# Fetching 32 columns of A per row for list tiles that belong to single groups

## The chip, the cores and the metric

The kernel runs on one core of a Trainium2 chip. The core has five engines with instruction queues of their own: TensorE (PE, with its weight loads shown apart as PEld), VectorE (DVE), ScalarE (ACT), GpSimd (POOL) and SyncE (SP). Sixteen DMA engines move data between the off-chip memory (HBM) and the on-chip memory (SBUF). The accumulators of TensorE lie in PSUM. The metric is the device time of one execution in microseconds (us). Three runs of the kernel before took 1524.8, 1528.96 and 1532.77 us; the median is 1528.96 us.

## The reference

Eight batches of 4096 nodes with 256 features pass through one layer of a graph network, a residual addition and a layer norm. The matrix `A` is 4096 x 4096 and mostly zero: node pairs with small numbers are connected often, those with large numbers rarely.

```python
HW = jnp.einsum('bnf,fo->bno', H, W)
A_norm = jax.nn.relu((A + A.T) * 0.5)
D = jnp.sum(A_norm, axis=1)
d_inv_sqrt = jnp.where(D > 0, D_safe ** (-0.5), 0.0)
DAD = d_inv_sqrt[:, None] * A_norm * d_inv_sqrt[None, :]
L_norm = jnp.eye(N, dtype=H.dtype) - DAD
out = jax.nn.relu(jnp.einsum('nm,bmo->bno', L_norm, HW))
x = _layernorm(x + out)
```

## The kernel before

**First stage, up to about 594 us.** The matrix is read in blocks of 512 x 512. TensorE transposes a block, VectorE adds it to its mirror block, ScalarE halves it and takes the positive part (`symmetrise` L464, `keep` L475). The result goes to `a_dram`, a table in HBM with 4096 rows of 4096 float32 values. VectorE also sums each row over groups of 32 columns (`sums`, L479, three buffers), and GpSimd notes in `uses` (L480) which groups of which rows hold anything. For blocks on the diagonal GpSimd copies the diagonal tile away (`diag`, L489). Beside this, TensorE forms the products of x and W, which are scaled by each row's root of the degree and written to `g_dram`: 4096 rows of 8 batches x 256 values, 8 KB each. `a_dram` and `g_dram` have one row more, of zeros, for places in a list that stay empty. The first 128 output rows are computed here with dense products (`lead`, L536).

Constant tables are filled at the very start. GpSimd writes the tables `kinds`, `limit` and `base` with one memset for every column (L184, L187, L188): 14 of the first and 224 of each other.

**Second stage.** The other 31 blocks of 128 output rows are handled in 16 units `u`, in the order `SEQ` (1 to 7, 0, 8 to 15). A unit has two blocks, `b` = 0 and 1 (output blocks 2u+1 and 2u+2); the last has one. A unit's 256 columns of A are eight groups of 32 (`E` = 32). Only rows of A that hold something in these columns have to be multiplied. They are sorted by the pattern of groups in which they hold something, the kinds: a kind is a mask of eight bits. The kinds 1, 2, 4, 8 (in block 0) and 16, 32, 64, 128 (in block 1) are single groups; 15 and 240 are a whole block; 51, 204, 60 and 195 are the same or crossed halves of both blocks; kind 0 takes the rest and needs all groups. Each kind has room for `CAPS[u][k]` slots of 64 rows, beginning with slot `FIRST[u][k]`. Two slots make a list tile of 128 rows. There are 268 list tiles, 10 to 27 to a unit. The rows 0 to 255 of A, which almost every column uses, are not listed: they are kept as `hubs` and multiplied whole (`gh`, L902).

The list of a unit is built on the chip, four units ahead of its use, mostly on VectorE (`patterns` L214, `place` L267, `place_rest` L350, `spread` L374). Its last steps are `collect` (L398), in which TensorE writes for every place of every tile the number of the row, in two parts, to PSUM, and `index` (L409), in which VectorE turns these into `gi`, the row of `g_dram`, and `ai`, the place in `a_dram`. `ai` is written in up to three pieces (L429) by the bounds of L123: first the tiles whose columns lie in block 0, then those of block 1, then those that need both. In the function `lists` (L1064) the steps of three units are put behind one another: `index` of one, then the scans of `place_rest` and of `place` of two later ones, which read the rest of the two PSUM banks that `lists` has borrowed from the accumulators of block 0. VectorE works through them in this order.

`gather` (L907) fetches a tile with two indirect DMAs on GpSimd's queue: the tile's columns of A into `ga` (L914) and its rows of g into `g` (L922). A row of `ga` is 128 columns (512 bytes), or 256 columns (1 KB) when both blocks need it. There is a ring of 12 buffers of each kind; `gather_ahead` (L932) issues the next pair as soon as the oldest tile's last product is behind. For most units the tiles of the next one are therefore on their way while this one is multiplied.

TensorE follows a list of 227 steps written out beforehand (`steps_of`, L789). A full step multiplies 128 rows by the 128 columns of one block, in four pieces of 512 values of g. A round has up to eight operations, each 64 rows by one group of 32 columns, by the same four pieces; the two halves of the rows and the four column groups lie side by side in the array. `product` (L1115) issues each matmul; its weights are `at[ps, off + cols.start : off + cols.stop]`, so a group's 32 columns are taken from the fetched 128 or 256.

When a block is done, ScalarE evicts it with the positive part and the row's factor (L731), VectorE adds x (L741), forms the statistics and normalises (L750 to L774), and SyncE's queue stores it. x is loaded from ScalarE's queue (L725) into four buffers, which the stores set free.

Of the kernel before, what the change touches and what calls it, by code (L numbers as in the profile page):

```python
# [2 lines left out]

# [8 lines left out]
ALU = mybir.AluOpType  # L12
AX = mybir.AxisListType
BF16 = mybir.dt.bfloat16
# [7 lines left out]
KINDS = [15, 1, 4, 2, 8, 16, 64, 32, 128, 240, 51, 204, 60, 195, 0]  # L22

SEQ = [1, 2, 3, 4, 5, 6, 7, 0, *range(8, 16)]
# [3 lines left out]
CAPS = [  # L28
# [18 lines left out]
FIRST = [  # L47
# [20 lines left out]
def kernel(  # L68
# [25 lines left out]
    nc = tc.nc  # L94
    B, N, F = x.shape
    FO = w.shape[1]
    P = 128
# [3 lines left out]
    NB = N // P  # L101
    FC = F // P
    G = B * FO
    NU = NB // 2
    Q = 64
    E = 32
    QU = P // E
    NE = 2 * QU
# [5 lines left out]
    NK = len(KINDS)  # L114
    L = 64
    mid = KINDS.index(16), KINDS.index(51)
    NL = NK - 1

    def upto_tile(u, ks):
        return max((FIRST[u][k] + CAPS[u][k] + 1) // 2 for k in ks)  # L120

    tiles = [upto_tile(u, range(NK)) for u in range(NU)]
    bounds = [(upto_tile(u, range(mid[0])), upto_tile(u, range(mid[1]))) for u in range(NU)]  # L123
    tmax = max(tiles)

    const = ctx.enter_context(tc.tile_pool(name="const", bufs=1))
# [15 lines left out]
    a_dram = dram.tile([N + 1, N], F32, name="a_dram")  # L142
# [42 lines left out]
    for u in SEQ:  # L185
        for k in range(NL):
            nc.gpsimd.memset(limit[:, u, k : k + 1], float(CAPS[u][k] * L))  # L187
            nc.gpsimd.memset(base[:, u, k : k + 1], float(FIRST[u][k] * L + 1))  # L188

    own = const.tile([P, NE, 2], F32, name="own")  # L190
    nc.vector.memset(own, 0.0)
    for s in range(NE):
        h = slice((s % QU) * E, (s % QU + 1) * E)
        nc.vector.memset(own[h, s, s // QU : s // QU + 1], 1.0)
    over = const.tile([P, NU], F32, name="over")

    def blocks(u):

        return min(2, NB - 1 - 2 * u)

    plan = {}

# [206 lines left out]
    def index(u, pl):  # L409
        t = tiles[u]  # L410

        low = ipool.tile([P, tmax], F32, tag="low", name=f"low_{u}")
        nc.vector.tensor_copy(low[:, :t], pl[:, 1, :])  # L413
        nc.vector.scalar_tensor_tensor(low[:, :t], pl[:, 0, :], float(P), low[:, :t], ALU.mult, ALU.add)
        gi = ipool.tile([P, tmax], U32, tag="gi", name=f"gi_{u}", bufs=3)
        nc.vector.tensor_scalar(gi[:, :t], low[:, :t], float(N), None, ALU.add)

        ai = ipool.tile([P, tmax], U32, tag="ai", name=f"ai_{u}", bufs=3)
        m0, m1 = bounds[u]
        if blocks(u) == 1:  # L420
            m0 = m1 = t
        for ts, n, k in (
            (slice(0, m0), NB, 2 * u + 1),
            (slice(m0, m1), NB, 2 * u + 2),
            (slice(m1, t), NU, u),
        ):
            if ts.start == ts.stop:
                continue
            nc.vector.tensor_scalar(  # L429
                ai[:, ts], low[:, ts], float(n), float(N * n + k), ALU.mult, ALU.add  # L430
            )
        plan[u] = gi, ai
        yield

# [8 lines left out]
    with (  # L443
# [219 lines left out]
        for i in range(NS):  # L663
# [37 lines left out]
            if i in (1, 2):  # L701
                for n, u in enumerate(SEQ[2 * i - 2 : 2 * i]):
                    at = 1 + 5 * n
# [79 lines left out]
    def store(i, z):  # L783
        nc.sync.dma_start(out[:, i * P : (i + 1) * P, :].rearrange("b p f -> p b f"), z)

    a_rows = a_dram.rearrange("j (c q) -> (j c) q", q=P)
    a_pairs = a_dram.rearrange("j (c q) -> (j c) q", q=2 * P)

# [67 lines left out]
    with (  # L856
# [8 lines left out]
        hubs = [  # L865
            gath.enter_context(tc.tile_pool(name=f"hub_{h}", bufs=1)).tile([P, G], F32, name=f"g_hub{h}")
            for h in range(max(HUBS))
        ]
        ring_rows = [apool.tile([P, 2 * P], F32, tag=f"a{k}", name=f"ga{k}") for k in range(RING)]
        hub_rows = [  # L870
            [apool.tile([P, P], F32, tag=f"h{h}{b}", name=f"gh{h}_{b}") for b in range(2)] for h in range(max(HUBS))
        ]
# [22 lines left out]
        def load_hub_rows(units, h, b):  # L895

            u = next((v for v in units if HUBS[v] > h), None)
            if u is None:
                return
            i = 2 * u + 1 + b  # L900
            with queue("pool"):
                nc.gpsimd.dma_start(  # L902
                    hub_rows[h][b], a_dram[h * P : (h + 1) * P, i * P : (i + 1) * P]
                )
            got[u, -1 - h, b] = (hub_rows[h][b], hubs[h], 0)

        def gather(n):  # L907

            u, t = order[n]
            both = t >= bounds[u][1]  # L910
            at, gt = ring_rows[n % RING], ring[n % RING]
            gi, ai = plan[u]
            with queue("pool"):
                nc.gpsimd.indirect_dma_start(  # L914
                    out=at if both else at[:, :P],
                    out_offset=None,
                    in_=a_pairs if both else a_rows,
                    in_offset=bass.IndirectOffsetOnAxis(ap=ai[:, t : t + 1], axis=0),
                    element_offset=P if both else 0,
                )  # L920
            with queue("pool"):
                nc.gpsimd.indirect_dma_start(  # L922
                    out=gt,
                    out_offset=None,
                    in_=g_dram,
                    in_offset=bass.IndirectOffsetOnAxis(ap=gi[:, t : t + 1], axis=0),
                    bounds_check=N if n < RING else N - 1,
                    oob_is_err=False,
                )
            got[u, t] = (at, gt, P if both else 0)  # L930

        def gather_ahead():  # L932
            nonlocal asked, eaten
# [181 lines left out]
        def product(u, op, c, ps, cols, start, stop):  # L1115

            t, _, b, _ = op
            at, gt, apart = got[u, t] if t >= 0 else got[u, t, b]
            off = b * apart
            with queue("pe"):  # L1120
                return nc.tensor.matmul(  # L1121
                    py[2 * u + 1 + b][c][cols, :],
                    lhsT=at[ps, off + cols.start : off + cols.stop],
                    rhs=gt[ps, c * S : (c + 1) * S],
                    start=start,
                    stop=stop,
                    skip_group_check=True,
                )
# [138 lines left out]
```

## Time and profile before

| What | Value |
|---|---|
| median of three runs | 1528.96 us |
| the profiled execution | 1529.14 us |
| its span, first to last instruction | 1527.3 us |
| TensorE busy | 1390.9 us (91%) |
| VectorE busy | 1040.8 us (68%) |
| GpSimd busy | 739.9 us (48%) |
| ScalarE busy | 363.7 us (24%) |
| moved by DMA | 550.64 MB, 361 GB/s on average |
| mean granted clock of TensorE | 0.964 of full |

The busy time of an engine is the time in which it has an instruction at work. Matmuls overlap, so a busy TensorE isn't a TensorE at its peak. "PEclk" is the clock granted to TensorE in tenths of full speed, and "DMA" is the mean busy share of the 16 DMA engines, in 40 equal slices of the span. A group row names line, engine, operation, output and inputs, shape and count, then its total time and the mean of one, and then the idle time of the engine before these instructions with what ended it.

### The profile page before, as it was taken

Reading aid. Unit: us, or ns where it says so; the run is one execution under the profiler, and the core shown is the slowest. Engines: PE = TensorE matmul, PEld = TensorE weight load, DVE = VectorE, ACT = ScalarE, POOL = GpSimd, SP = SyncE. Lnnn points to the kernel's source line nnn. Section 1 sums busy time; section 2 is a strip of 40 time slices with the busy share of each in tenths; the row PEclk is TensorE's granted clock in tenths of the full one; section 3 lists DMA queues with packets and bytes.
Section 4 is the critical chain, followed back from the end, with each engine's and each line's share of the span. In section 5 each row is a group of like instructions: output and inputs, shape, how many; then the busy total and the mean of one; then the engine's idle time right before and its main releaser. Section 6 shows DMA issues by size and latency. Waiting matters only on the chain.

```text
span 1527.3 us, 29344 instructions
## 1 busy us (share of the span) xinstructions
PE 1390.9 (91%) x11008; PEld 753.8 (49%) x11008; DVE 1040.8 (68%) x3135; ACT 363.7 (24%) x462; POOL 739.9 (48%) x1264
## 2 busy tenths in 40 slices
PE   6999998989989987999999999999899998989883
PEld 5878877777777752343433333333233333333331
DVE  6676578979955454109586797789109988999354
ACT  3555544544544440000101101100001010101111
POOL 4002010011303324766775776776556776777661
PEclk9999999999999988899999999999899999999996
DMA  9999999999989997998999999999978999999994
GB/s 352 361 362 398 392 371 355 359 350 358 351 308 352 340 403 263 398 411 320 389 366 382 368 391 374 409 368 362 415 269 285 371 392 400 386 380 384 408 364 156
DMA packets 217924, 550.64 MB, mean 361 GB/s; under 512 B 19369, under 2 KB 107737, under 8 KB 183193
## 3 DMA queue, kind: packets, MB, share of 16 engines
q0 software_dynamic: 55392, 290.44, 48.7%
q1 hardware_dynamic: 93472, 126.89, 24.2%
q10 hardware_dynamic: 68912, 131.37, 22.8%
q8 instruction: 89, 1.46, 0.4%
q14 instruction: 59, 0.48, 0.1%
HBM read 445.64 MB, written 136.34 MB: 381 GB/s over the span
## 4 chain that ended last, share of the span: by engine, by line
PE 50%; DMA 23%; DVE 16%; issue 6%; POOL 3%; ACT 2%; SPq 0%; ACTq 0%; POOLq 0%; DVEq 0%
PE py L1121 31%; DMA g<-g_dram,gi 9%; PE pg L578 9%; PE lead L536 5%; DMA a_dram<-sym 4%; DVE sym L472 3%; DMA out_dram<-xr 3%; PE tr L468 3%; DMA xin<-in_x_dram 3%; PE xtr L567 3%; DVE sums L479 2%; DMA ga<-a_dram,ai 2%; POOL ga L914 2%; DMA adj<-in_adj_dram 1%; DVE stats L750 1%
## 5 line engine op out<-in xcount | busy, mean ns | idle before, releaser
L1121 PE MATMUL py<-g,ga 64*32 64x512 f32 (+1 forms) x7136 | 627.0, 608 | 41.3 <-DMA g<-g_dram,gi 34.3
L1121 PEld LDWEIGHTS py<-g,ga 64*32 64x32 f32 (+1 forms) x7136 | 229.2, 113 | 422.8 <-issue 333.8
L922 POOL DMA_INDIRECT g<-g_dram,gi x268 | 299.6, 1118 | 117.5 <-issue 57.6
L914 POOL DMA_INDIRECT ga<-a_dram,ai x268 | 285.6, 1066 | 139.7 <-PE py L1121 69.8
L731 ACT ACTIVATE y<-py,minus_r 128x512 f32<-128x512 f32 x120 | 74.9, 688 | 808.5 <-PE py L1121 608.4
L578 PE MATMUL pg<-w_sb,xt 128*128 128x256 f32 x1024 | 229.2, 382 | 5.8 <-ACT xt L568 4.0
L1121 PE MATMUL py<-g_hub,gh 128*128 128x512 f32 x480 | 220.7, 601 | 5.0 <-DVE pos_k L210 5.0
L472 DVE TENSOR_TENSOR sym<-tr,adj 128x512 f32<-128x512 f32 x256 | 162.1, 681 | 73.9 <-PE tr L468 72.3
L578 PEld LDWEIGHTS pg<-w_sb,xt 128*128 128x128 f32 x1024 | 193.6, 192 | 33.5 <-ACT xt L568 4.4
L480 POOL TENSOR_SCALAR uses<-sums 128x64 uint8<-128x64 f32 x64 | 27.6, 431 | 346.7 <-DVE sums L479 308.4
L479 DVE TENSOR_REDUCE sums<-sym 128x64 f32<-128x2048 f32 x64 | 145.3, 2277 | 54.9 <-ACT sym L476 54.9
L468 PE MATMUL tr<-ident,adj 128*128 128x128 f32 x1024 | 140.3, 288 | 29.5 <-DVE sym L472 16.3
L1121 PEld LDWEIGHTS py<-g_hub,gh 128*128 128x128 f32 x480 | 87.6, 190 | 132.7 <-issue 118.2
L476 ACT ACTIVATE sym<-sym 128x2048 f32<-128x2048 f32 x64 | 122.8, 1918 | 127.5 <-DVE sym L472 127.5
L413 DVE COPY low<-lists 128x17 f32<-128x17 f32 (+8 forms) x14 | 2.4, 174 | 221.1 <-PE lists L401 221.1
L468 PEld LDWEIGHTS tr<-ident,adj 128*128 128x128 f32 x1024 | 120.5, 147 | 56.1 <-DVE sym L472 31.5
L741 DVE TENSOR_TENSOR xr<-xr,y 128x2048 f32<-128x2048 f32 x31 | 70.9, 2286 | 61.4 <-ACT y L731 29.3
L750 DVE BATCH_NORM_STATS2 stats<-xr 128x6 f32<-128x256 f32 x256 | 87.0, 412 | 1.1
L567 PE MATMUL xtr<-ident,xin 128*128 128x128 f32 x512 | 72.1, 290 | 16.5 <-DVE sym L472 14.0
L774 DVE TENSOR_SCALAR xr<-xr,mv,root 128x256 f32<-128x256 f32 x248 | 83.9, 409 | 0.5
L536 PE MATMUL lead<-gt,strip 128*128 128x512 f32 x176 | 82.6, 593 | 0.0
L380 DVE TENSOR_TENSOR hot<-iota_q,at 128x1024 bf16<-128x1024 f32 x64 | 74.4, 1217 | 7.2 <-DMA a_dram<-sym 7.2
(152 smaller groups left out, 1025.9 us busy)
## 6 DMA issues: line engine op xcount, KB each, us to landing
adj<-in_adj_dram SPq DMA_DIRECT2D x64, 1024.0 KB, 11.8
a_dram<-sym ACTq DMA_DIRECT2D x64, 1024.0 KB, 9.7
out_dram<-xr SPq DMA_DIRECT2D x31, 1024.0 KB, 23.4
xr<-in_x_dram ACTq DMA_DIRECT2D x29, 1024.0 KB, 20.4
xin<-in_x_dram SPq DMA_DIRECT2D x44, 512.0 KB, 12.6
g_dram<-gt ACTq DMA_DIRECT2D x22, 1024.0 KB, 8.5
xin<-in_x_dram POOLq DMA_DIRECT2D x20, 512.0 KB
g_dram<-held ACTq DMA_DIRECT2D x10, 1024.0 KB, 11.5
```

The lines of the kernel that those rows point to most:

```text
L468: ins = nc.tensor.transpose(pt[:, c * P : (c + 1) * P], tji[:, c, a * P : (a + 1) * P], ident)
L472: nc.vector.tensor_add(sym[:, a, :], pt, tij[:, a, :])
L476: nc.scalar.activation(sym, sym, AF.Relu, scale=0.5)
L479: nc.vector.tensor_reduce(sums, sym.rearrange("p a (c q) -> p a c q", q=E), AX.X, ALU.add)
L536: nc.tensor.matmul(lead[c], lhsT=strip, rhs=g[:, c * S : (c + 1) * S], start=not done, stop=len(done) == NB - 1, skip_group_check=True,)
L567: nc.tensor.transpose(pt[:, k, c, :], xin[b // H][:, b % H + k, c * P : (c + 1) * P], ident)
L578: ins = nc.tensor.matmul(pg[:, k * FO : (k + 1) * FO], lhsT=xt[:, b + k, c, :], rhs=w_sb[:, c, :], start=(c == 0), stop=(c == FC - 1),)
L750: nc.vector.bn_stats(stats[:, b, :], z[:, b, :])
L774: nc.vector.tensor_scalar(z[:, b, :], z[:, b, :], mv[:, b, 0:1], rstd[:, b : b + 1], ALU.subtract, ALU.mult,)
L914: nc.gpsimd.indirect_dma_start(out=at if both else at[:, :P], out_offset=None, in_=a_pairs if both else a_rows, in_offset=bass.IndirectOff ...
L922: nc.gpsimd.indirect_dma_start(out=gt, out_offset=None, in_=g_dram, in_offset=bass.IndirectOffsetOnAxis(ap=gi[:, t : t + 1], axis=0), boun ...
L1121: return nc.tensor.matmul(py[2 * u + 1 + b][c][cols, :], lhsT=at[ps, off + cols.start : off + cols.stop], rhs=gt[ps, c * S : (c + 1) * S], ...
```

## The change

For each list tile a table made when the program is built, `owner`, says whose columns it holds: 0 or 1 for one block, 2 for both, and 3 (`ALONE`) when every slot of the tile belongs to a kind of a single group. The two slots of such a tile may belong to different groups. 155 of the 268 tiles are of this sort, 45 others hold columns of one block and 68 those of both.

For an `ALONE` tile each place fetches just the 32 columns of its slot's group, 128 bytes, through a view of `a_dram` in pieces of 32 columns. The piece's number within the row differs by half of the tile, so `index` adds it from a new table `group_of` (128 x 16 x 11, bf16), which GpSimd fills at the start: one memset of the whole and 299 memsets of half a column. `ai` is now written in runs of neighbouring tiles of the same sort, 83 pieces over all units in place of 46. The row's offset N (the lists hold j - N) is added in the first operation of `index` and no longer in the third and in each piece of `ai`. In `product` the weights of an `ALONE` tile are the columns 0 to 31 of `ga`. The shapes of the matmuls, the number of gathers and the number of rows stay.

```diff
+    def owners(u, t):
+        kinds_at = [k for k in range(NK) for s in (2 * t, 2 * t + 1) if FIRST[u][k] <= s < FIRST[u][k] + CAPS[u][k]]
+        masks = [KINDS[k] or 255 for k in kinds_at]
+        if all(m & (m - 1) == 0 for m in masks):
+            return ALONE
+        both = blocks(u) == 2
+        return max(2 if both and m & 15 and m >> QU else int(m & 15 == 0) for m in masks)
+    ALONE = 3
+    owner = [[owners(u, t) for t in range(tiles[u])] for u in range(NU)]
+    alone = [[t for t in range(tiles[u]) if owner[u][t] == ALONE] for u in range(NU)]
...
+    group_of = const.tile([P, NU, max(map(len, alone))], BF16, name="group_of")
+    nc.gpsimd.memset(group_of, 0.0)
+    for u in SEQ:
+        for n, t in enumerate(alone[u]):
+            for i in range(2):
+                for k in range(1, 1 + NE):
+                    if FIRST[u][k] <= 2 * t + i < FIRST[u][k] + CAPS[u][k]:
+                        g = QU * (2 * u + 1) + KINDS[k].bit_length() - 1
+                        nc.gpsimd.memset(group_of[i * L : (i + 1) * L, u, n : n + 1], float(g))
...
-        nc.vector.tensor_copy(low[:, :t], pl[:, 1, :])
+        nc.vector.tensor_scalar(low[:, :t], pl[:, 1, :], float(N), None, ALU.add)
         nc.vector.scalar_tensor_tensor(low[:, :t], pl[:, 0, :], float(P), low[:, :t], ALU.mult, ALU.add)
-        nc.vector.tensor_scalar(gi[:, :t], low[:, :t], float(N), None, ALU.add)
+        nc.vector.tensor_copy(gi[:, :t], low[:, :t])
...
+        for who, run_of in groupby(range(t), lambda k: owner[u][k]):
+            run_of = list(run_of)
+            ts = slice(run_of[0], run_of[-1] + 1)
+            if who == ALONE:
+                k = group_of[:, u, n : n + len(run_of)]
+                nc.vector.scalar_tensor_tensor(ai[:, ts], low[:, ts], float(N // E), k, ALU.mult, ALU.add)
+                n += len(run_of)
+            else:
+                rows, k = (NU, u) if who == 2 else (NB, 2 * u + 1 + who)
+                nc.vector.tensor_scalar(ai[:, ts], low[:, ts], float(rows), float(k), ALU.mult, ALU.add)
...
+    a_groups = a_dram.rearrange("j (c q) -> (j c) q", q=E)
     a_rows = a_dram.rearrange("j (c q) -> (j c) q", q=P)
...
+            both, one = owner[u][t] == 2, owner[u][t] == ALONE
...
-                    out=at if both else at[:, :P],
+                    out=at if both else at[:, : E if one else P],
-                    in_=a_pairs if both else a_rows,
+                    in_=a_pairs if both else a_groups if one else a_rows,
...
-            off = b * apart
+            off = -cols.start if one else b * apart
```

More of the change, by code (lines that the diff above doesn't have):

```diff
@@ L1 @@
 from contextlib import ExitStack, nullcontext
-from itertools import chain
+from itertools import chain, groupby
 import concourse.bass as bass
@@ L117, with blocks @@
     NL = NK - 1
+    def blocks(u):
+        return min(2, NB - 1 - 2 * u)
     def upto_tile(u, ks):
@@ L122 @@
     tiles = [upto_tile(u, range(NK)) for u in range(NU)]
-    bounds = [(upto_tile(u, range(mid[0])), upto_tile(u, range(mid[1]))) for u in range(NU)]
+    def owners(u, t):
[8 more added lines that the diff above has]
+    alone = [[t for t in range(tiles[u]) if owner[u][t] == ALONE] for u in range(NU)]
     tmax = max(tiles)
@@ L195 @@
     over = const.tile([P, NU], F32, name="over")
-    def blocks(u):
-        return min(2, NB - 1 - 2 * u)
     plan = {}
@@ L412, in index @@
         low = ipool.tile([P, tmax], F32, tag="low", name=f"low_{u}")
-        nc.vector.tensor_copy(low[:, :t], pl[:, 1, :])
+        nc.vector.tensor_scalar(low[:, :t], pl[:, 1, :], float(N), None, ALU.add)
         nc.vector.scalar_tensor_tensor(low[:, :t], pl[:, 0, :], float(P), low[:, :t], ALU.mult, ALU.add)
         gi = ipool.tile([P, tmax], U32, tag="gi", name=f"gi_{u}", bufs=3)
-        nc.vector.tensor_scalar(gi[:, :t], low[:, :t], float(N), None, ALU.add)
+        nc.vector.tensor_copy(gi[:, :t], low[:, :t])
         ai = ipool.tile([P, tmax], U32, tag="ai", name=f"ai_{u}", bufs=3)
[L419 to L431, printed above, removed]
+        n = 0
+        for who, run_of in groupby(range(t), lambda k: owner[u][k]):
[8 more added lines that the diff above has]
+                nc.vector.tensor_scalar(ai[:, ts], low[:, ts], float(rows), float(k), ALU.mult, ALU.add)
         plan[u] = gi, ai
@@ L904, in load_hub_rows @@
                 )
-            got[u, -1 - h, b] = (hub_rows[h][b], hubs[h], 0)
+            got[u, -1 - h, b] = (hub_rows[h][b], hubs[h], 0, False)
         def gather(n):
             u, t = order[n]
-            both = t >= bounds[u][1]
+            both, one = owner[u][t] == 2, owner[u][t] == ALONE
             at, gt = ring_rows[n % RING], ring[n % RING]
@@ L929, in gather @@
                 )
-            got[u, t] = (at, gt, P if both else 0)
+            got[u, t] = (at, gt, P if both else 0, one)
         def gather_ahead():
@@ L1117, in product @@
             t, _, b, _ = op
-            at, gt, apart = got[u, t] if t >= 0 else got[u, t, b]
-            off = b * apart
+            at, gt, apart, one = got[u, t] if t >= 0 else got[u, t, b]
+            off = -cols.start if one else b * apart
             with queue("pe"):
```

## The prediction

> **What bounds the kernel now.** I read the page first, its busy slices and DMA queues, and then the groups of the second stage (594 us to the end).
>
> ```profile
> PE   6999998989989987999999999999899998989883
> DMA  9999999999989997998999999999978999999994
> q0 software_dynamic: 55392, 290.44, 48.7%
> L1121 PE MATMUL py<-g,ga 64*32 64x512 f32 (+1 forms) x7136 | 627.0, 608 | 41.3 <-DMA g<-g_dram,gi 34.3
> L922 POOL DMA_INDIRECT g<-g_dram,gi x268 | 299.6, 1118 | 117.5 <-issue 57.6
> L914 POOL DMA_INDIRECT ga<-a_dram,ai x268 | 285.6, 1066 | 139.7 <-PE py L1121 69.8
> ```
>
> TensorE and the 16 DMA engines are both nearly full from end to end, so the page alone doesn't say which is the limit. GpSimd isn't: a pair of gathers takes it about 2.6 us with its gaps, and 268 pairs are some 690 us of 907. I cut the second stage at the first matmul of each unit. The rows are: length, then busy us with instruction counts of PE, PEld, DVE, ACT and POOL, then granted clock, DMA share, GB/s.
>
> ```profile
> 688.00:753.00 65.00, 65.00 (x598) 25.33 (x597) 44.68 (x168) 4.84 (x8) 41.74 (x40) 1.00 0.94 350
> 753.00:814.00 61.00, 61.00 (x613) 23.60 (x612) 41.62 (x156) 4.84 (x8) 44.30 (x42) 1.00 1.00 378
> ...
> 1145.00:1191.00 46.00, 43.80 (x566) 16.67 (x564) 43.68 (x167) 4.84 (x8) 30.55 (x29) 1.00 0.82 289
> 1191.00:1243.00 52.00, 47.96 (x461) 19.38 (x446) 46.53 (x170) 5.17 (x8) 40.44 (x38) 0.97 1.01 379
> 1243.00:1291.00 48.00, 44.98 (x493) 18.10 (x493) 41.51 (x156) 5.19 (x8) 33.48 (x33) 0.96 1.03 402
> 1291.00:1338.00 47.00, 43.94 (x467) 17.45 (x464) 44.14 (x166) 5.17 (x8) 33.08 (x33) 1.00 1.02 387
> 1338.00:1386.00 48.00, 43.35 (x473) 17.30 (x469) 45.12 (x164) 4.84 (x8) 36.34 (x34) 0.96 1.02 384
> 1386.00:1436.00 50.00, 42.50 (x400) 17.63 (x401) 28.41 (x99) 4.84 (x8) 36.76 (x35) 0.93 1.01 396
> ```
>
> Units 2 and 3 (first two rows) keep PE wholly busy: there DMA is hidden. Unit 8 has spare DMA. Units 9 to 13 (last five) have DMA at 1.01 to 1.03 while PE falls back: there DMA is the limit. To put a size on it I took, from the trace's matmul records, the time from one step's first matmul to the next step's. An undisturbed full step takes 3.53 us and a round 3.43 to 3.6; what is over that is a stall. Stalls at rounds that take newly gathered tiles: unit 4 2.9 us, unit 6 4.7, unit 7 2.3, unit 0 13.3, unit 9 8.1, unit 10 5.0, unit 11 2.2, unit 12 5.9, unit 13 1.9, unit 15 9.4; together 56 us. (The first round of unit 1 stalls 16 us more, while GpSimd issues the first pairs one by one; DMA size doesn't set that.) Units 2, 3, 5, 8 and 14 show none of this kind worth counting. So at most 56 us of the run can answer to lighter gathers.
>
> **The DMA saving.** From CAPS and FIRST, 155 of the 268 list tiles hold single groups only; 45 others fetch 512 B a row and 68 fetch 1 KB. All 128 rows of a tile still come, so the number of gathers, of rows, and GpSimd's issues stay. Bytes fall by 155 x 128 x 384 = 7.6 MB of the page's 550.64 MB, 1.4%.
>
> What does a gather cost the engines? The trace's packet records, by size, have median durations of 9 ns at 4 B, 27 at 512 B, 46 at 1,024 B, 84 at 2,048 B, 159 at 4,096 B and 309 at 8,192 B: 8.5 ns plus bytes at 27 B/ns. The 512 B gather of 128 rows appears as 16 packets of 4,096 B, eight rows each, one per engine, and in the second stage such packets average 174 ns. Eight rows in one packet cost no more than its bytes: 18.8 ns a row.
>
> The trace of before has no 128 B rows. New cost of a gather on each engine, from the nearest rows:
> - lowest: a 1,024 B packet, priced by bytes, 46 ns;
> - each row pays the fixed 8.5 ns of a small packet and its bytes: 8 x (8.5 + 4.7) = 106 ns;
> - each row costs what a 512 B row does: 159 ns, no gain;
> - highest: eight lone 512 B packets, 8 x 27 = 216 ns; as an outer bound twice the present packet, 318 ns.
>
> I take 77 ns, eight rows at the fixed 8.5 ns each (which then hides the 4.7 ns of bytes) and one packet's 8.5: the 4 B packets at 9 ns are the nearest rows for a piece that small. That saves 174 - 77 = 97 ns a gather.
>
> The Trainium skill's page "DMA: Bandwidth & Descriptors" speaks against the change: its Specifications put line rate at 512 B and more, with a read-modify-write below. Read as a doubling of the byte price this would be 92 ns, saving 6.4 us on the 78 gathers counted below. The same page, "Why small descriptors are slow", gives a fixed 3 cycles over 32 B beats; my estimate from it is 7 beats against 19, 59 ns, saving 9.0 us. No row of before shows either.
>
> **How much reaches the end.** Alone tiles gathered ahead of a stall in their unit: units 9 to 13 and 15 have 11 + 9 + 10 + 10 + 8 + 8 = 56, with DMA full up to the stall, so I count all. Units 4, 6, 7 and 0 have 11 + 10 + 11 + 11 = 43 with DMA shares of 0.91 to 0.98, so backlog isn't continuous: half, 22. That is 78 x 97 ns = 7.6 us. No unit's saving (about 1 us) exceeds its stall. If every one of the 155 counted it would be 15.0 us; late next would be the full steps of PE, which have 3.53 us each whatever is fetched.
>
> **What is added.**
>
> ```profile
> 20.16 0.10 POOL L187 MEMSET limit<- 128x1 f32 x1
> 20.19 0.10 POOL L188 MEMSET base<- 128x1 f32 x1
> 20.23 1.00 POOL L489 COPY diag<-sym 128x128 f32<-128x128 f32 x4
> 21.25 0.39 POOL L480 TENSOR_SCALAR uses<-sums 128x64 uint8<-128x64 f32 x1
> ...
> 1292.29 0.31 DVE L429 TENSOR_SCALAR ai<-low 128x6 uint32<-128x6 f32 x3
> 1292.51 0.21 DVE L206 TENSOR_TENSOR_SCAN incl_r<-carry,lists 128x32 f32<-128x32 bf16 x1
> ```
>
> GpSimd's table: one memset of the whole and 299 of a column half, behind limit and base. They start 33 ns apart (20.16 to 20.19), so 9.9 us. GpSimd is already late here: sym (0,0) is ready at 13.7 us, its diagonal is copied at 20.2. The copies then end near 31.2 instead of 21.2; the next writer of that sym buffer is VectorE's 13th add at 30.63, which the chain of waits passes through. TensorE's products (23.2 to 30.1) cover all but +0.65 us; without that cover it would be 9.9. `uses` comes near 31.6, ahead of the fourth sums (37.7) that needs its buffer.
>
> VectorE's index: the three operations before ai change kind, not number, at 0.17 us each. ai goes from 46 pieces to 83, by runs of like tiles. Three took 0.22 us from start to start of what follows (1292.29 to 1292.51), so 2.3 more a unit are about 0.2 us. Behind them in VectorE's order stand the scans that free the two list banks of PSUM for the next unit. TensorE waits there in three units (12.5 us in six waits on pos_k), so about +0.7 us; elsewhere the other block's products hide it. Bounds: nothing, and 37 x 0.21 us = 7.8 us if each were exposed unpipelined. The table is written some 400 us before its first use at 449 us and adds no wait. The matmuls keep their shapes (32 columns of lhsT, now from column 0): 0; were PE slower there, nothing would hide it.
>
> **Sum.** -7.6 + 0.65 + 0.7 = -6.2 us. The profiled execution took 1529.14 us, 0.2 above the median of the runs, so 1523 us, 0.4% less.
>
> **Rivals.**
> 1. Priced by bytes: 46 ns. 78 to 110 gathers save 128 ns: 10 to 14 us, less 1.4: 1516 to 1521. For it: medians linear in bytes. Against it: no packet made of pieces under 512 B.
> 2. Nothing moves: rows cost the same (159 ns), or the saving is refilled by the stores and loads beside it. Additions remain: 1529 to 1531. For it: 18.8 ns a row is only an upper bound for a smaller one.
> 3. Slower: a 128 B row costs more than a 512 B row. From 191 ns a packet (24 ns a row) the loss of 17 ns on 78 gathers adds to the 1.4; at 318 ns it is 78 x 0.144 + 1.4 = 12.6 us, and with all 155 24 us: 1532 to 1553. It passes 0.5% at 254 ns. Against it: semaphore writes of 4 B at 9 ns. For it: DMA is full, nothing would hide it.
>
> **Numbers.** About 0.5% (7.6 us) is what a measurement of this kernel can tell from no change. Forecast (60 to 110 ns on 78 to 100 gathers; 1519 to 1526, its own range) 0.40: of it 0.14 faster, 0.26 same. Rival 1 0.24: 0.20 faster, 0.04 same. Rival 2 0.13: 0.10 same, 0.03 slower. Rival 3 0.23: 0.20 slower, 0.03 same. Faster 0.34, same 0.43, slower 0.23. The range leaves out the ends of rivals 1 and 3: 1512 to 1538.
>
> **What would show it.** Packet records: 155 x 16 packets of 1,024 B on q0, at 60 to 110 ns (right), 46 (rival 1), 159 or more (rivals 2, 3); or 128 B packets, if rows aren't joined. Bytes 7.6 MB lower. Stalls of units 9 to 13 shorter by about 1 us each, units 2 and 3 unchanged. Diagonal copies near 30.2 us. 83 ai rows. Wrong would make it: rows at a higher price; a store or a residual load that lands later and holds ScalarE's queue (its evictions waited 71.3 us on stores); stalls that come back elsewhere.

## The result and the profile after

The changed kernel takes 1549.54 us (median of 6 runs, 1547.51 to 1552.21); the kernel before, beside it, 1527.24 us (6 runs). The ratio is 1.0142, with a 95% interval of 1.0124 to 1.016: the change makes the kernel 1.4% slower. The forecast was 1523.0 us, with a range up to 1538.

I cut both profiled executions at the first and the last matmul of the second stage:

| | before | after | difference |
|---|---|---|---|
| first matmul of the second stage, us | 593.6 | 622.4 | +28.8 |
| from there to the stage's last matmul, us | 906.8 | 896.8 | -10.0 |
| whole span, us | 1527.3 | 1545.8 | +18.5 |

So there are two effects of opposite sign. The stage with the lighter gathers became 10.0 us shorter. But it begins 28.8 us later, and ahead of it the change adds only a table and, from 478 us on, some pieces of `ai`.

The page of the changed kernel, its busy slices, queues and main groups:

```profile
PE   5399998979898989699999999999899999999792
POOL 7402101010222322774777677766755777777661
DMA  9299999999989897999999899999987999999994
q0 software_dynamic: 55392, 282.82, 47.3%
L1142 PE MATMUL py<-g,ga 64*32 64x512 f32 (+1 forms) x7136 | 621.3, 605 | 30.5 <-DMA g<-g_dram,gi 24.5
L943 POOL DMA_INDIRECT g<-g_dram,gi x268 | 303.9, 1134 | 111.6 <-issue 61.8
L935 POOL DMA_INDIRECT ga<-a_dram,ai x268 | 286.8, 1070 | 129.8 <-PE py L1142 56.8
```

The second slice of 38 us is the place: PE falls from 9 to 3 and the DMA engines from 9 to 2, while everything behind is as full as before. q0 has the same number of packets and 7.6 MB less, as predicted, and the matmuls waited 10.8 us less (30.5 instead of 41.3).

What fills that slice stands in GpSimd's timeline (start, time taken, instruction, and in brackets the idle time before it):

```profile
20.02 0.10 POOL L204 MEMSET base<- 128x1 f32 x1
20.05 0.24 POOL L207 MEMSET group_of<- 128x176 bf16 x1
20.36 38.67 POOL L214 MEMSET group_of<- 64x1 bf16 x299
59.09 1.00 POOL L509 COPY diag<-sym 128x128 f32<-128x128 f32 x4
```

The 299 small memsets take 38.67 us, not 9.9. They start 133 ns apart (median), though one is shown as lasting about as long as those of `limit` and `base`, which start 33 ns apart. The copies of the diagonal tile behind them come at 59.09 us instead of 20.23. VectorE's and TensorE's timelines show who stands behind these copies:

```profile
60.13 0.69 DVE L492 TENSOR_TENSOR sym<-tr,adj 128x512 f32<-128x512 f32 x1 [34.42 <-POOL diag L509]
```

```profile
30.72 2.05 PE L488 MATMUL tr<-ident,adj 128*128 128x128 f32 x16
60.87 1.12 PE L488 MATMUL tr<-ident,adj 128*128 128x128 f32 x4 [28.10 <-DVE sym L492]
```

VectorE's 13th add, which overwrites the `sym` buffer that the copies read, starts at 60.13 us instead of 30.63, where before it had waited for TensorE:

```profile
30.63 0.69 DVE L472 TENSOR_TENSOR sym<-tr,adj 128x512 f32<-128x512 f32 x1 [5.70 <-PE tr L468]
```

TensorE's next transposes wait for this add, 28.10 us. The DMA engines idled most of the time as well. This is the stretch from 26 to 60 us before, with a DMA share of 1.00, and then after (columns as in the prediction's rows by unit):

```profile
26.00:60.00 34.00, 31.50 (x178) 27.18 (x178) 19.77 (x25) 19.10 (x23) 1.47 (x4) 0.95 1.00 354
26.00:60.00 34.00, 6.77 (x39) 5.75 (x37) 0.00 (x0) 3.78 (x5) 24.77 (x261) 0.66 0.36 136
```

Blocks of the matrix that weren't loaded in this time are loaded later. The first stage keeps its DMA engines full in nearly every slice, so it has no room to make the time good, and nearly all of the wait is still there at 622 us.

The second stage by units, which answers to the prediction's rows:

```profile
717.00:782.00 65.00, 65.00 (x597) 25.17 (x596) 44.80 (x169) 4.85 (x8) 40.78 (x40) 1.00 0.93 343
782.00:843.00 61.00, 61.00 (x613) 23.70 (x612) 41.52 (x157) 4.85 (x8) 45.59 (x42) 1.00 0.99 374
1168.00:1216.00 48.00, 45.37 (x565) 16.76 (x564) 45.58 (x173) 4.85 (x8) 32.37 (x32) 0.96 0.83 291
1216.00:1265.00 49.00, 46.31 (x452) 18.40 (x445) 44.11 (x168) 5.18 (x8) 36.53 (x35) 0.97 1.00 362
1265.00:1313.00 48.00, 46.26 (x511) 18.85 (x509) 42.08 (x157) 5.18 (x8) 35.63 (x35) 0.96 1.03 402
```

These are units 2, 3, 8, 9 and 10. Units 2 and 3, which TensorE fills, are as long as before. Unit 9, with DMA full, went from 51.4 to 49.2 us and unit 10 from 48.6 to 47.6; by the same cut units 4, 6, 7, 0, 9 to 13 and 15, the ones with stalls, became 12.2 us shorter together. Unit 8, which had DMA to spare, became 1.9 us longer, and all units without stalls 2.2 us together. These are single executions, and one unit's length moves by up to 3 us without any narrow row: in e17 below, where units 9, 10 and 15 keep their wide rows, they were 1.3 us shorter, 3.2 longer and 2.3 shorter than before.

The packet records on q0 give the price of a narrow gather: 2,480 packets of 1,024 B, which is 155 x 16. The eight rows of 128 B that go to one DMA engine are joined in one packet, with a median of 46 ns and a mean of 57. 46 ns is also what a 1,024 B packet took before.

### The profile page after: what moved, and what is told of

It reads as the page before. It is cut to its first block, busy times and chain, and to the rows that moved or that the text cites. A ratio compares the mean times of both kernels' runs of the same rounds, so it can differ in the third digit from the quotient of the medians.

```text
span 1545.8 us, 29684 instructions
## 1 busy us (share of the span) xinstructions
PE 1390.2 (90%) x11008; PEld 753.5 (49%) x11008; DVE 1042.8 (67%) x3172; ACT 363.8 (24%) x462; POOL 773.5 (50%) x1564
## 4 chain that ended last, share of the span: by engine, by line
PE 46%; DVE 22%; DMA 19%; issue 6%; POOL 5%; ACT 2%; ACTq 0%; SPq 0%; DVEq 0%; POOLq 0%
PE py L1142 26%; PE pg L598 8%; DMA g<-g_dram,gi 7%; PE lead L556 5%; DVE sym L492 3%; DMA a_dram<-sym 3%; DMA out_dram<-xr 3%; PE xtr L587 3%; PE tr L488 3%; DVE sums L499 3%; DMA ga<-a_dram,ai 2%; DVE stats L770 2%; POOL group_of L214 2%; DMA xin<-in_x_dram 2%; DVE xr L761 1%
## 5 line engine op out<-in xcount | busy, mean ns | idle before, releaser
L1142 PE MATMUL py<-g,ga 64*32 64x512 f32 (+1 forms) x7136 | 621.3, 605 | 30.5 <-DMA g<-g_dram,gi 24.5
L1142 PEld LDWEIGHTS py<-g,ga 64*32 64x32 f32 (+1 forms) x7136 | 225.3, 113 | 410.9 <-issue 333.8
L943 POOL DMA_INDIRECT g<-g_dram,gi x268 | 303.9, 1134 | 111.6 <-issue 61.8
L588 ACT COPY xt<-xtr 128x512 f32<-128x512 f32 x128 | 68.0, 593 | 44.6 <-PE xtr L587 43.5
## 6 DMA issues: line engine op xcount, KB each, us to landing
xr<-in_x_dram ACTq DMA_DIRECT2D x29, 1024.0 KB, 19.9
```

Of the source, the lines that this page charges most:

```text
L943: nc.gpsimd.indirect_dma_start(out=gt, out_offset=None, in_=g_dram, in_offset=bass.IndirectOffsetOnAxis(ap=gi[:, t : t + 1], axis=0), boun ...
L1142: return nc.tensor.matmul(py[2 * u + 1 + b][c][cols, :], lhsT=at[ps, off + cols.start : off + cols.stop], rhs=gt[ps, c * S : (c + 1) * S], ...
```

## The experiments

Theory A: the table alone costs the 28.8 us, because a memset whose partitions differ from those of the one before it waits for that one; the lighter gathers save about 10 us. Rivals: each small memset is slow for another reason (its size, its type, its 64 partitions); or the late start comes from something else in the change; or the second stage is shorter only because it starts later.

Experiments e1 to e11 ran on two chips where the kernel before itself took 1760 to 1767 us; in the profiles of e1 and e5 the second stage starts at 594 us as here, but lasts some 240 us longer. e12 to e17 ran on two chips where the kernel before took 1527.7 and 1529.3. Each is compared with the kernel before on the same chip, and sizes in the second stage are taken from the later ones.

### The table alone, and the change without its table's price

**e3, the table alone.** The kernel before, with the table filled and never read:

```diff
+    group_of = const.tile([P, NU, max(map(len, alone))], BF16, name="group_of")
+    nc.gpsimd.memset(group_of, 0.0)
+    for u in SEQ:
+        for n, t in enumerate(alone[u]):
+            for i in range(2):
...
+                        nc.gpsimd.memset(group_of[i * L : (i + 1) * L, u, n : n + 1], float(g))
```

> The kernel before with the table filled at the start as in the change, but never used: rows of A are fetched with 128 columns as before. If the table costs what the start of the second stage shows, 1527.2 + 28.8 = 1556 us (1553 to 1559), with an unchanged second stage of about 934 us. If the loss comes from elsewhere in the change, 1527 us.

Measured: 1794.55 us against 1767.12, ratio 1.0168 [1.0111, 1.0225], which is 27.4 us (20 to 40 by the interval, from four executions). The second stage starts at 621.6 us. GpSimd's timeline, the table's end and the copies behind it:

```profile
54.97 3.96 POOL L214 MEMSET group_of<- 64x1 bf16 x30
59.00 1.01 POOL L511 COPY diag<-sym 128x128 f32<-128x128 f32 x4
```

The copies come within 0.1 us of where the full change has them. The table by itself makes the late start.

**e1, the table by halves.** The full change, with the same 299 memsets in another order: all lower halves first, then all upper halves.

```diff
-    for u in SEQ:
-        for n, t in enumerate(alone[u]):
-            for i in range(2):
+    for i in range(2):
+        for u in SEQ:
+            for n, t in enumerate(alone[u]):
```

> The changed kernel with the 299 small memsets of the table in another order: first all that write partitions 0 to 63, then all that write 64 to 127. Theory A (a memset that writes other partitions than the one before it has to wait for that one to end, 133 ns instead of 33): the table takes about 10 us instead of 38.6, the diagonal copies start near 30.4 us instead of 59.1, the second stage starts near 595 us instead of 622, and the kernel takes 1517 to 1522 us. Theory B (a memset of 64 partitions or of 2 bytes a partition costs 133 ns in any order): nothing changes, about 1549 us. Theory C (the lost time is not the table's): about 1549 us, whatever the memsets take.

Measured: 1768.66 us against 1767.12, ratio 1.002 [0.9992, 1.0049]; the second stage starts at 594.2 us. GpSimd's timeline, and then VectorE's:

```profile
19.95 3.32 POOL L214 MEMSET group_of<- 64x1 bf16 x99
23.83 4.37 POOL L214 MEMSET group_of<- 64x1 bf16 x128 [0.55 <-issue]
28.81 2.43 POOL L214 MEMSET group_of<- 64x1 bf16 x72 [0.61 <-issue]
31.30 1.00 POOL L509 COPY diag<-sym 128x128 f32<-128x128 f32 x4
```

```profile
32.34 0.69 DVE L492 TENSOR_TENSOR sym<-tr,adj 128x512 f32<-128x512 f32 x1 [8.62 <-POOL diag L509]
```

The same memsets now start 34 ns apart and take 11.3 us with the gaps between the batches. Only their order was changed, so a memset of 64 partitions and one bf16 column isn't slow by itself. Here the forecast's picture of the start nearly comes true: copies at 31.30 us, where it had 30.2, and an add that is 1.7 us late, where it had 0.65.

**e10 and e11, change and halves beside each other.** On one chip, the full change and the same by halves:

> The changed kernel as it is, on the chip of these runs. If its loss is the table at the start and the rest makes no difference here: 27 to 29 us over the kernel before, as e3 (the table alone).

> The kernel of e1 beside e10 on the same chip: 27 to 29 us less than e10. Against the kernel before: no difference where the second stage waits for TensorE (a chip on which the kernel before takes about 1760 us), 1517 to 1522 us where it takes about 1527.

Measured: the change 1786.48 us, by halves 1766.57, before 1761.4; ratios 1.013 [1.0055, 1.0205] and 1.002 [0.9982, 1.0058]. The order of the memsets is worth 19.9 us between these medians, less than the expected 27 to 29; with four executions of the change this is known to some 10 us either way. The change's +25 us shows that its loss is there on this chip too; whether the narrow rows gain there can't be read from intervals this wide.

**e15, by halves where the kernel before takes 1529 us.**

> The changed kernel with the memsets of the table sorted by halves, where the kernel before takes about 1527 us: as e14 (1520 us) plus the 0.7 us by which the diagonal copies still come late, 1518 to 1524 us. If the order of the memsets doesn't help here, about 1549 us.

Measured: 1525.96 us against 1529.33, ratio 0.9976 [0.9963, 0.9989]. That is 2 us above the top of the expected 1518 to 1524. The second stage starts at 597.3 us, 3.7 later than in the profile of before, and lasts 898.1. The table ends later than hoped:

```profile
20.52 3.32 POOL L214 MEMSET group_of<- 64x1 bf16 x99
24.43 4.37 POOL L214 MEMSET group_of<- 64x1 bf16 x128 [0.59 <-issue]
29.70 2.43 POOL L214 MEMSET group_of<- 64x1 bf16 x72 [0.90 <-issue]
32.20 1.00 POOL L509 COPY diag<-sym 128x128 f32<-128x128 f32 x4
```

VectorE's add starts at 33.23 us, 2.6 late. So even at 33 ns the table in this place would have cost somewhat more than the 0.65 us of the prediction: the cover ends at 30.6 us, and the gaps between the batches (0.59 and 0.90 us) and the late beginning add to the memsets.

### What makes the memsets slow

**e4, six tables.** In the kernel before, six unused tables are filled with memsets of one column each: bf16 halves in turn, lower halves only, upper halves only, all partitions, float32 halves in turn, and lower half and all partitions in turn.

```diff
+        tab = const.tile([P, 32], dt, name=name)
+        for n in range(32):
+            for h in halves:
+                nc.gpsimd.memset(tab[h, n : n + 1], float(n))
```

> The kernel before with six unused tables filled at the start by memsets of one column each, to read the distance from one memset to the next: bf16 with halves in turn (0 to 63, 64 to 127), bf16 only lower half, bf16 only upper half, bf16 all partitions, float32 with halves in turn, bf16 with the lower half and all partitions in turn. Theory A: 33 ns where the partitions stay the same (second, third, fourth table), 133 ns where they change (first, fifth, sixth). Theory B1 (64 partitions are slow): 133 ns in the first, second, third, fifth. Theory B2 (2 bytes are slow): 133 ns in all but the fifth.

GpSimd's timeline, one row per table:

```profile
19.90 8.50 POOL L201 MEMSET t_alt<- 64x1 bf16 x64
28.44 1.12 POOL L201 MEMSET t_low<- 64x1 bf16 x32
29.59 1.12 POOL L201 MEMSET t_high<- 64x1 bf16 x32
30.77 1.17 POOL L201 MEMSET t_all<- 128x1 bf16 x32
31.82 8.38 POOL L201 MEMSET t_f<- 64x1 f32 x64
40.24 2.17 POOL L201 MEMSET t_mix<- 64x1 bf16 x64
```

From start to start (medians): 134, 34, 34, 34, 131 and 34 ns. Halves in turn are slow in both types; one half again and again isn't. The sixth table is a miss for theory A as I had it: its memsets cover 64 and 128 partitions in turn, a different set each time, and run at 34 ns. Both begin at partition 0. What costs the 100 ns is a change of the *first* partition of the output. The seams between the tables say the same, and show that it isn't a matter of sets without a common partition: partitions 64 to 127 (third table, its last memset ends at 30.71) are followed by 0 to 127 (fourth, begins at 30.77 us), which overlap but begin elsewhere, and the new one starts behind the old one's end. From the fourth table to the fifth, both from partition 0, the new one starts (31.82) before the old one ends (31.94). Only 0 and 64 were tried as first partitions on GpSimd.

The Trainium skill, page "VectorE: DVE Perf Modes", section "Two Vector instructions with no wait between them", has a rule of this form for another engine: a Vector instruction whose output begins in another group of 32 partitions than the last one's is held until every earlier Vector instruction has finished. The page states no such rule for GpSimd; the six tables are what shows it there.

The trace of before held a row of this kind, on VectorE:

```profile
1.84 0.73 DVE L194 MEMSET own<- 32x1 f32 x8
```

Eight memsets of 32 partitions that begin at 0, 32, 64 and 96 in turn take 0.73 us; in the trace they start 91 to 99 ns apart and last 59. It was the nearest row to the new table by the pattern of its partitions; I priced the table by the nearest rows on the same engine, `limit` and `base`, which all begin at partition 0.

### The change with its table out of the way

**e2 and e5, ten memsets at a time behind each `uses`.** The table's first use is near 450 us, so it can be written in small pieces, each behind an instruction of GpSimd that runs beside the first stage anyway:

```diff
-                        nc.gpsimd.memset(group_of[i * L : (i + 1) * L, u, n : n + 1], float(g))
+                        fills.append((group_of[i * L : (i + 1) * L, u, n : n + 1], float(g)))
...
-            nc.gpsimd.tensor_scalar(
+            ins = nc.gpsimd.tensor_scalar(
...
+            with tc.issue_after(ins.ins):
+                for to, g in fills[:10]:
+                    nc.gpsimd.memset(to, g)
+                fills[:10] = []
```

> The changed kernel with the same memsets in the same order, but ten at a time behind the note of each block in uses, so that the diagonal copies do not wait for them. If the table at the start costs the 28.8 us by which the second stage began later, and lighter gathers save 10.3 us of the second stage: 1527.2 - 10.3, so 1515 to 1520 us, with the second stage starting near 594 us. If the shorter second stage was only a consequence of the later start (or of other orders), 1525 to 1530 us.

> The kernel of e2 once more, to see its second stage where the DMA engines, and not TensorE, bind the kernel before. On a chip on which the kernel before takes about 1527 us: 1515 to 1520 us, the second stage 10 us shorter than before (a stage of 923 us against 934), with the stalls of units 0, 6, 9 and 15 shorter. If the shorter second stage of the changed kernel was only a consequence of its later start, 1525 to 1530 us. On a chip on which the kernel before takes about 1767 us and its rounds wait for TensorE: no difference beyond the interval.

Measured: 1772.96 against 1767.12 us, 1.0022 [0.9985, 1.006]; and 1763.62 against 1759.91, 1.003 [0.9997, 1.0063]. In e2 the second stage starts at 592.4 us, so the late start is gone, but the gain of 10 us doesn't show on these chips.

**e14, the same kernel where the kernel before takes 1528 us.**

> The kernel of e2 a third time. Where the kernel before takes about 1527 us: 1515 to 1520 us. Where it takes about 1760 us: no difference beyond the interval.

Measured: 1519.98 us against 1527.66, ratio 0.9942 [0.9924, 0.9961]. This is 7.7 us less than the kernel before (6.0 to 11.6 by the interval), at the edge of the expected 1515 to 1520. The second stage starts at 594.7 us, 1.1 later than in the trace of before, and lasts 900.4, 6.4 less, so the lighter gathers shorten it by themselves. GpSimd's timeline, then VectorE's:

```profile
20.28 1.00 POOL L514 COPY diag<-sym 128x128 f32<-128x128 f32 x4
21.97 0.39 POOL L501 TENSOR_SCALAR uses<-sums 128x64 uint8<-128x64 f32 x1 [0.69 <-DVE sums L500]
22.32 1.29 POOL L506 MEMSET group_of<- 64x1 bf16 x10
```

```profile
31.35 0.69 DVE L493 TENSOR_TENSOR sym<-tr,adj 128x512 f32<-128x512 f32 x1 [5.70 <-PE tr L489]
```

The copies are back at 20.28 us, and the add waits for TensorE's transposes as it did before, with the same 5.70 us. Ten memsets take 1.29 us, still some 130 ns each, but here nobody waits for them.

### Where the gathers' saving counts

The prediction counted the units with stalls (4, 6, 7, 0, 9 to 13, 15) and gave nothing to those that TensorE or a list fills (2, 3, 5, 8, 14; unit 1 joins them here, since its stall is set by GpSimd). e16 takes the late table and keeps narrow rows only in the first set, 99 tiles; e17 only in the others, 56 tiles:

```diff
+    SOME = (0, 4, 6, 7, 9, 10, 11, 12, 13, 15)
...
-        if all(m & (m - 1) == 0 for m in masks):
+        if u in SOME and all(m & (m - 1) == 0 for m in masks):
```

> Narrow rows only in units 0, 4, 6, 7, 9 to 13 and 15 (99 of 155 tiles), the table filled late. If only gathers ahead of stalls count: the whole gain of e14, 1518 to 1522 us. If each counts the same: 64% of 7.7 us, about 1523 us. On a chip where the kernel before takes about 1760 us: no difference.

> Narrow rows only in units 1, 2, 3, 5, 8 and 14 (56 of 155 tiles), the table filled late. If only gathers ahead of stalls count: no gain, 1526 to 1529 us. If each counts the same: 36% of 7.7 us, about 1525 us.

Measured beside one another, before 1529.33 us: the stalled units 1522.61, ratio 0.9962 [0.9945, 0.9978]; the others 1528.82, ratio 0.999 [0.9974, 1.0006]. In absolute times e16 lies between its two forecasts, and e17 in that of no gain. The medians gain 6.7 and 0.5 us, where shares in proportion to the tiles would be 4.6 and 2.6. Each interval alone would still allow that. Side by side the two kernels differ by 6.2 us in the medians (5.6 in the means, give or take 3.3 at 95%), where shares in proportion would differ by 2.0.

From its first to its last matmul the second stage took 897.4 and 907.6 us, where the trace of before has 906.8; but the profiled execution of e16, 1515.99 us, was the fastest of its nine, so its 9.4 us are too many. A steadier sign is the prediction's own measure, the time that rounds of the ten units with stalls take beyond an undisturbed one (here all rounds over 3.9 us, by what they exceed 3.55): 54 us before, 36 in the changed kernel, 39 in e14, 40 in e16 and 53 in e17. So nearly all of the gain is in the 99 tiles of the stalled units. Not all that the rounds lose is won: of 18 us in the changed kernel, 12.2 are left in the length of these units, so the rest came back at other steps.

The first try of this pair, on chips where the kernel before takes 1760 us, told nothing apart:

> The kernel of e5, but narrow rows only in the units in which the kernel before stalled for gathers (0, 4, 6, 7, 9 to 13, 15: 99 of the 155 tiles). If only DMA time taken from those stalls counts: all of the gain of e5, about -10 us against the kernel before (1515 to 1520 us). If each narrow gather counts the same wherever it lies: 64% of it, about -6.5 us. On a chip whose second stage waits for TensorE: no difference.

> The kernel of e5, but narrow rows only in the units in which TensorE was busy throughout or DMA had time to spare (1, 2, 3, 5, 8, 14: 56 of the 155 tiles). If only DMA time taken from stalls counts: no gain, 1525 to 1529 us. If each narrow gather counts the same: 36% of the gain of e5, about -3.7 us.

Measured: 0.997 [0.9938, 1.0003] and 1.0011 [0.9978, 1.0044].

### What a narrow gather is worth where nothing hides it

**e12 and e13, a second stage bound by DMA from end to end.** Both kernels issue only a quarter of the second stage's matmuls of full steps and rounds, so that TensorE is never the limit: e12 is the kernel before, e13 the one with the late table.

```diff
-                for c in range(NC):
+                for c in range(1 if hs <= begun else NC):
...
-                for m in range(NC):
+                for m in range(1):
```

> The kernel before, with three quarters of TensorE's second-stage work left out: after the first full step of a block each step multiplies only the first of its four pieces of g (a round's upper rows the third), so most of the sum is missing. Gathers, loads and stores stay. DMA should bind the second stage: its packets sum to 889 us there, so 1480 to 1520 us and a DMA share near 1.0.

> The same work left out, with the narrow rows and the table filled as in e2. Against e12: every narrow gather counts where DMA binds throughout, 155 x (174 - 57 ns) = 18 us less. If narrow rows cost the engines as much as rows of 512 bytes: no difference. If the stage is bound by something else (GpSimd's issues, 740 us; the stores): no difference and a DMA share under 0.95.

Measured: 1502.09 and 1488.65 us, a difference of 13.4. The ratios to the kernel before, 0.9817 [0.979, 0.9844] and 0.9717 [0.968, 0.9754], leave some 7 us either way, so the expected 18 isn't excluded. The second stage takes 881.9 and 868.5 us, the same 13.4. Its main part, as windows of e12 and then of e13:

```profile
626.00:1460.00 834.00, 552.85 (x2529) 145.88 (x2526) 593.76 (x2209) 73.72 (x118) 603.43 (x568) 0.73 1.00 383
```

```profile
626.00:1460.00 834.00, 558.89 (x2549) 147.00 (x2546) 603.10 (x2264) 73.68 (x118) 605.71 (x571) 0.72 1.00 380
```

The DMA share is 1.00 in both, so here every gather counts: 13.4 us over 155 tiles is 86 ns a gather. The packet records fit the smaller figure. From 5 us ahead of the stage's first matmul to the end of its last, the packets sum to 879.5 us for each engine in e12 and 866.5 in e13, 13.0 less. The packets of 4,096 and 1,024 B on q0, the gathers of A and what else has these sizes, became 17.2 us shorter together; those of 8,192 B, which are rows of g, took 329.4 ns on average instead of 327.3, 4.0 us more. Why the rows of g take longer isn't shown, nor, with one profile of each, that they always do.

**e8 and e9, half of each matmul's columns,** were meant for the same question and missed it. In both, all matmuls but the first of a group use 256 of their 512 columns.

```diff
+                n = S if start else S // 2
...
-                    py[2 * u + 1 + b][c][cols, :],
+                    py[2 * u + 1 + b][c][cols, :n],
```

> The kernel before with less for TensorE to do in the second stage: every product after the first of its accumulators adds only 256 of the 512 columns of g, so half of the sum is left out. Gathers, loads and stores stay. It is the base of e9: with TensorE relieved, the DMA engines should bind the second stage on any chip. From the kernel before's DMA time in that stage (889 us summed over the packets) and its unfilled start and end: 1470 to 1520 us, the stage's DMA share near 1.0. If the slower second stage of e1 to e7 was not TensorE's doing, it stays above 1700 us.

> The same with the narrow rows, the table filled as in e2 (late). Against e8: if every narrow gather counts where DMA binds, 155 x (174 - 57 ns) = 18 us less; if only half of them count, 9 us; if narrow rows cost the engines as much as rows of 512 bytes, no difference.

Measured: 1594.25 and 1601.23 us against 1761.4, ratios 0.9049 [0.8987, 0.9112] and 0.9084 [0.9026, 0.9141]: no gain from narrow rows. Neither forecast of e8 holds: 1594 us is above 1520 and below 1700. But the DMA share from 626 to 1460 us was 0.94 and 0.92, so DMA wasn't the limit all along, and these two runs say nothing on the price of a narrow row.

## Why the prediction was wrong

**The step that failed** is the price of the table: "They start 33 ns apart (20.16 to 20.19), so 9.9 us". They start 133 ns apart and took 38.67 us, and the term of the sum that rests on it, +0.65 us, measured +28.8. The pitch was read from `limit` and `base`, which differ from the new memsets in the one thing that sets it: they begin at the same partition every time, while the table's rows begin at 0 and 64 in turn (e1, e4).

**The cover was named rightly, and was too short.** "TensorE's products (23.2 to 30.1) cover all but +0.65 us; without that cover it would be 9.9" has the right buffer, the right waiting add and the right place. Cover up to about 30 us hides 10 us of table and not 38.7; the add came 29.5 us late, and 28.8 of them reached the second stage. With the table at 33 ns (e1, e15) the same term was 1.7 to 2.6 us. None of the three rivals had the table as its mechanism. Rival 3 gave a slower kernel and even times that hold the measured one, but by dear narrow rows, which the packets rule out.

**The price of a narrow gather** was taken at 77 ns on each engine; the records show 46 in the median and 57 in the mean, which is rival 1's price. Rows of 128 B are joined and paid by their bytes; the fixed 8.5 ns for every row isn't there (packet records of the changed kernel). The doubling below 512 B that I read into the Trainium skill ("DMA: Bandwidth & Descriptors", Specifications; 92 ns) isn't seen in these packets; the estimate from the same page's "Why small descriptors are slow" (59 ns) lies near the mean of 57 and above the median of 46.

**What of it reaches the end** was counted rightly in the main: the units with stalls gained (12.2 us in the profile; e16), the full ones nothing (e17). Units 9 to 13, which were to gain about 1 us each, changed by -2.2, -1.0, -0.7, +0.5 and -0.1. That the tiles of units 4, 6, 7 and 0 count by half was not tested. With the measured 57 ns, the prediction's own 78 gathers give 78 x 117 ns = 9.1 us, against 10.0 measured over the stage, where 7.6 was predicted. That agreement is partly luck: the two executions profiled lie 2.0 us below and 1.9 above their medians, and over the stage the packets of 4,096 and 1,024 B on q0 became 17.5 us lighter for each engine, while the rows of g became 6.0 heavier. The medians of e14, without the late start, give 7.7 us, where the prediction's -7.6 and +0.7 leave 6.9.

**VectorE's index** was put at +0.7 us in TensorE's waits on `pos_k`, from "12.5 us in six waits". They are three stalls, each seen twice at the same moment, by the matmuls (5.0 us together) and by their weight loads (7.5). They grew to 6.0 and 8.4 us, so by about 1.0 and not by the sum of both. The place, the banks of the lists, was the right one, and `ai` has 83 pieces as worked out.

Put together with the measured terms: +28.8 for the start, -10.0 for the second stage with VectorE's share in it, -0.3 behind it, +18.5 us of span. The medians differ by 22.3 us; the profiled execution of after was the fastest of its six (1547.51 us), and that of before lay 1.9 above its median, which is the other 3.9.

## What to carry to other kernels

The duration in a row isn't the distance to the next instruction: before a price is multiplied by 299, it must come from instructions that follow one another as the new ones will, on the same partitions and in the same order. An added block of set-up costs what its queue holds up, and cover ends at a definite time; here one change of loop order, or ten pieces at a time behind work that runs anyway, took away the 28.8 us. Here a saving in DMA time counted in the units where TensorE stalls on DMA and hardly elsewhere, and those units can be listed from the trace before anything is built.

## What the runs showed beyond that

- GpSimd's memsets start 34 ns apart when their outputs begin at the same partition, and 131 to 134 ns apart when the first partition changes each time between 0 and 64. It was so in bf16 and in float32, and 64 and 128 partitions in turn, both from 0, cost nothing more (e4).
- On two chips the second stage of the same program took about 240 us longer, while the first stage took the same 594 us. SyncE's queue waits no longer for matmuls in e1 than before (855.5 us; 890.1 before), but also for something that the profile doesn't name, which the trace of before doesn't show:

```profile
SPq L1209 <- PE py L1142: 855.5, 357, 74.7
SPq L1209 <- remote: 281.6, 63, 14.7
```

  The DMA engines are less full there, as in this window of unit 9 (DMA share 0.84, clock 0.82, where the changed kernel above has 1.00 and 0.97), so the gathers' time on the engines doesn't explain it. Several expectations above take TensorE for the limit on these chips; no run shows that, and the cause stays open. The gain of the late table, which e14 shows, doesn't appear there (e2, e5).

```profile
1370.00:1438.00 68.00, 50.36 (x452) 18.02 (x444) 43.11 (x168) 5.17 (x8) 37.29 (x37) 0.82 0.84 293
```

- A low granted clock doesn't by itself mark a long run: in e12 and e13 it was 0.73 and 0.72 in the windows above, with TensorE idle a third of the time, and those were the shortest runs of all.
